# Layer-normed graph kernel of two layers: four small moves in the order of its first pairs and of its last one

## The chip, the cores and the metric

The kernel runs on one core of a Trainium2 chip. The metric is the device time of one execution in microseconds. Before the change it is 1700.62 us (median of three runs, 1700.39 to 1701.86).

## The reference, cut to what matters

There are 64 graphs of 256 nodes with 512 features, in fp32. Every graph uses the same adjacency matrix of zeros and ones, about 3% of them ones. Two layers follow each other; each normalises, clips at zero, mixes and adds to its input.

```python
# layer 0
h = maximum(layernorm(x), 0)
q, k, v = h @ Wq.T, h @ Wk.T, h @ Wv.T
rel = adj.T * (q @ k.T)                       # per graph, 256 x 256
rel = rel / norm(rel, axis=2, keepdims=True)
x = x + rel @ v
# layer 1
h = maximum(layernorm(x), 0)
x = x + (adj @ h) @ weight + bias
```

## The kernel before

**Tiling.** The graphs are worked in 32 pairs. A pair's x is one tile of 128 partitions by four chunks of 512 (two graphs, two halves of their nodes), 1 MB. Five such tiles form a ring (`x_ring`), so a pair's x is loaded several pairs ahead.

**Algebra.** Wq and Wk are folded into one matrix M once, in `before_pairs`, so that the scores are h M h transposed. Nearly all products are done by Strassen's scheme in Winograd's form: seven block products instead of eight, with sums of blocks formed ahead (`left_factors`, L176 to L179, and `right_operands`, L138 to L141) and added up afterwards. A product of blocks goes to one PSUM bank; its `take` copies it (ScalarE, first time) or adds it (VectorE) to the result. `bank_a` is used for several products one after the other; a product that starts `bank_a` afresh or goes on in it waits until the take before it has read the bank. `two_levels` goes one level deeper for some of the blocks (steps named a1, c5, a6, c, a7, a4 and g1 to g4).

**Before the pairs.** `before_pairs` loads adj, Wq and Wk, computes M from seven products and meanwhile prepares pair 0. With `early=True` the seven come in the order 1, 2, 5, 6, 3, 7, 4; they are called first to seventh product below, and the banks are a, b, c, a, c, a, a. The first and third, fourth and seventh are taken by ScalarE's copy, the second, fifth and sixth by VectorE's addition. The rest of the preparation is: the statistics of pair 0 (L333, L334), their root on ScalarE (L338), reciprocal and shift `nb` (L341, L342), four Relus into `blocks` (L345), and Wv turned by 16 transposes on TensorE into four banks (`transpose_wv`). After the branch on `low_any` (whether adj is exact in a shorter format, which it is here) pair 0's h is turned by 16 transposes (`transposes_by_matmul`), copied to `ht` by four copies of ScalarE (L434), and multiplied with M (`project_g`); the second product of that stage, in bank_c, needs L177, which needs all four copies.

**Order of the work.** TensorE, VectorE and ScalarE run in the order in which the program writes their instructions (`manual_schedule`). The order is laid out by hand: a dictionary `side` tells which small steps follow which product. `run_steps` runs product n and its take, then the steps listed under n. So an instruction on VectorE or ScalarE that must wait holds up all that is listed behind it. The order on GpSimd and SyncE (SP) is left to the scheduler; DMAs are issued from the queues of SP, ScalarE and GpSimd.

**Loads at the start.** SP issues Wq in four parts and then x of pair 0; ScalarE issues adj and then Wk in four parts. Wv is issued by ScalarE after the copy of the first product, x of pairs 1 and 2 later.

**Pairs 0 and 1.** `first_pairs` fills the pipeline. Its last stage runs `mix_and_v(0, ...)`: the product of pair 0's gathered h with the weight (steps of m, additions L786 and L537 to x) between products for pair 2. Meanwhile pair 1's scores, which sixteen small DMAs have placed by blocks of 32 (L592, `placed`), are turned by four transposes of VectorE (`turns`, L602), and L176 to L179 form sums of them for the attention of pair 1, which follows (`attend_and_v`, L675 and L682).

**The last pair.** `last_pairs` empties the pipeline. There the last pair's layer 1 is done while the pair before is mixed: Relus (L345), a split of h in two terms by ScalarE's cast (L720) and VectorE's subtraction (L724), the addition of the bias to x (`add_bias`, L736, four chunks on GpSimd), the gather with adj (`y_products`, L752, copied by L756) and the mixing with the weight. The bias may be added as soon as a chunk's Relu has read x, and must be there before the first L786 of that pair.

Of the kernel before, what the change touches and what calls it, by code (L numbers as in the profile page):

```python
# [19 lines left out]
def kernel(  # L20
# [38 lines left out]
    nc = tc.nc  # L59
    P = 128  # L60
    B, N, D = x.shape
# [38 lines left out]
    for e in range(DC):  # L100
        nc.sync.dma_start(out=wq_sb[:, e], in_=wq[e * P : (e + 1) * P, :])
        nc.scalar.dma_start(out=wk_sb[:, e], in_=wk[e * P : (e + 1) * P, :])
    load(0)
    ones = const.tile([P, 1], F32, name="ones")
# [625 lines left out]

    def add_bias(i):

        xt = flat(X[i])
        add = nc.gpsimd.tensor_tensor
        return [
            (lambda c=c: add(xt[:, c, :], xt[:, c, :], bias_bc, ALU.add)) for c in range(TC)  # L736
        ]
# [95 lines left out]
    def before_pairs():  # L833
# [36 lines left out]
        def transpose_wv():  # L870
            for d in range(DC):
                pt = ps_m.tile([P, 512], F32, tag="pm", name="ptw")
                for e in range(DC):
                    nc.tensor.transpose(pt[:, ts(e, P)], wv_sb[:, e, ts(d, P)], ident)
                if d < HC:
                    nc.scalar.copy(wvt_sb[:, d, :], pt[:, :D])
                else:
                    nc.vector.tensor_copy(wvt_sb[:, d, :], pt[:, :D])

        def take(t, k, bank, first):  # L880
# [11 lines left out]
            0: [load_wv, left_steps[2], right_steps[2]],  # L892
            1: [left_steps[3], left_steps[0]],
            2: [right_steps[0]] + stats[0:1] + [lambda: load(1, nc.scalar)],
            3: stats[1:4] + [root, lambda: load(2, nc.scalar)],
            4: [end] + relus + [right_steps[3]],
            5: m_steps[0:3] + [transpose_wv],
            6: m_steps[3:4],
# [48 lines left out]
    def first_pairs(exact):  # L947
# [50 lines left out]
        if exact:  # L998
# [14 lines left out]
            0: y_steps[2:4] + totals[0:2], 1: y_second[0:4] + totals[2:4],  # L1013
            2: y_second[4:8] + [mean] + row_squares[0:2], 3: v_steps[1:2] + row_squares[2:4],
            4: turns + rel_steps[0:2] + norm0[0:2], 5: rel_steps[2:4] + v_steps[2:3],
        })
# [51 lines left out]
    def last_pairs(exact, relu0, v_last, mixed, v):  # L1068
# [62 lines left out]
            0: [root], 1: y_second[0:4] + [end] + relus[0:2] + uppers[0:2], 2: y_second[4:8],  # L1131
            4: lowers[0:2] + relus[2:4], 5: uppers[2:4] + add_bias(c), 7: lowers[2:4],
        })
        y_products, y_steps = gather_steps(c, exact)
        run_steps(y_products, {0: [m["g4"]], 2: y_steps[0:1]})
        y_second = second_of_y(c, "hs2")
# [42 lines left out]
```

## Time and profile before

| | |
|---|---|
| median of three runs | 1700.62 us |
| the profiled execution's own time | 1700.89 us |
| its span, first to last instruction | 1699.1 us |
| TensorE, matmul busy | 1685.2 us (99%) |
| VectorE busy | 1474.9 us (87%) |
| ScalarE busy | 856.7 us (50%) |
| GpSimd busy | 227.1 us (13%) |
| TensorE busy, 0 to 30 us | 26.48 us |
| TensorE busy, 30 to 1610 us | 1578.31 us |
| TensorE busy, 1610 to 1699 us | 80.41 us |
| mean granted TensorE clock | 0.999 |

How to read it. The profile is of one execution, and durations and points in time are those of that execution; time counts from the start of its span. L12 is line 12 of the kernel before. Engines are PE (TensorE), PEld (its weight loads), DVE (VectorE), ACT (ScalarE), POOL (GpSimd) and SP; a q behind a name is that engine's queue, where it issues DMAs. A row of a timeline names the output and the input of an instruction. An fp32 matmul leaves two records, so a product of four matmuls is counted as x8. A wait is put down to what came last by semaphores. A busy TensorE is not one at its peak; the idle time between its instructions is what can be read for sure.

### The profile page before, as it was taken

To read this page: it belongs to the slowest core of one execution; us is meant where nothing else is said; L and a number is where in the kernel's file an instruction comes from. 1 tells how busy PE (TensorE), PEld (TensorE's weight loads), DVE (VectorE), ACT (ScalarE), POOL (GpSimd) and SP (SyncE) were. 2 spreads that over 40 slices of the span, in tenths; PEclk is the share of its full clock that TensorE was granted. 3 is DMA by queue.
4 is the path that set the end of the run, shared out by engine and by line. 5 is a ranking of instruction groups with operands and counts; after the bars stand their busy time and mean duration, and the time that the engine had idled before them with its cause. 6 is when DMAs were issued, how large, how long until landed. Compare 5 with 4: busy or idle time off the path is not lost.

```text
span 1699.1 us, 28457 instructions
## 1 busy us (share of the span) xinstructions
PE 1685.2 (99%) x10274; PEld 1530.6 (90%) x10274; DVE 1474.9 (87%) x3312; ACT 856.7 (50%) x1947; POOL 227.1 (13%) x191
## 2 busy tenths in 40 slices
PE   9999999999999999999999999999999999999998
PEld 7988999999999999999999999999999999999986
DVE  7788898888898888898888988888988889888777
ACT  4455445655545555446555456554465544564331
POOL 1211100111101111001111011110011110011111
PEclk9999999999999999999999999999999999999999
DMA  7413332233322233322333322333223333223101
GB/s 245 63 28 85 83 77 51 47 82 85 78 60 64 52 84 85 75 55 57 67 85 81 77 48 49 85 84 76 57 64 58 84 82 78 51 44 60 38 25 53
DMA packets 395270, 118.89 MB, mean 70 GB/s; under 512 B 367600, under 2 KB 368368, under 8 KB 395120
## 3 DMA queue, kind: packets, MB, share of 16 engines
q1 hardware_dynamic: 382528, 76.60, 24.1%
q0 software_dynamic: 8432, 32.51, 5.2%
q10 hardware_dynamic: 4160, 7.87, 1.3%
q8 instruction: 83, 1.36, 0.3%
q14 instruction: 67, 0.55, 0.1%
HBM read 38.27 MB, written 33.55 MB: 42 GB/s over the span
## 4 chain that ended last, share of the span: by engine, by line
PE 96%; DVE 3%; DMA 0%; issue 0%; ACT 0%; ACTq 0%; DVEq 0%
PE bank_a L302 25%; PE bank_a L290 13%; PE bank_a L314 7%; PE py L752 7%; PE bank_c L302 7%; PE bank_e L528 6%; PE bank_a L675 6%; PE bank_d L528 5%; PE bank_c L290 3%; PE bank_c L314 3%; PE bank_e L481 3%; PE bank_c L675 3%; PE bank_d L481 2%; PE bank_b L314 2%; PE bank_b L675 1%; PE pu L636 1%
## 5 line engine op out<-in xcount | busy, mean ns | idle before, releaser
L736 POOL TENSOR_TENSOR x_ring<-x_ring,bias_bc 128x512 f32<-128x512 f32 x128 | 187.6, 1486 | 667.6 <-DVE rel L563 436.3
L302 PE MATMUL bank_a<-wv_t,ht 128*128 128x256 f32 x768 | 181.7, 379 | 0.0
L290 PE MATMUL bank_a<-ht,m_t 128*128 128x256 f32 x768 | 181.4, 379 | 0.0
L290 PEld LDWEIGHTS bank_a<-ht,m_t 128*128 128x128 f32 x768 | 145.9, 190 | 19.8
L302 PEld LDWEIGHTS bank_a<-wv_t,ht 128*128 128x128 f32 x768 | 143.5, 190 | 18.3
L516 ACT COPY v<-bank_a 128x512 f32<-128x512 f32 x96 | 55.1, 574 | 206.5 <-PE bank_a L302 206.5
L724 DVE TENSOR_TENSOR h<-h2c,h 128x512 fp32r<-128x512 f32 x128 | 85.5, 691 | 80.1 <-ACT h L720 80.1
L367 ACT ACTIVATE blocks<-x_ring,sm 128x512 f32<-128x512 f32 x112 | 80.9, 722 | 119.4 <-DVE sm L364 117.6
L345 ACT ACTIVATE h2c<-x_ring,nb,rs 128x512 f32<-128x512 f32 x128 | 97.3, 808 | 59.7 <-DVE nb L342 50.0
L752 PE MATMUL py<-adjt_r,h 128*128 128x256 f32 x1024 | 126.0, 280 | 0.5 <-DVE h L724 0.4
L302 PE MATMUL bank_a<-w_t,ys 128*128 128x256 f32 x512 | 121.4, 380 | 0.4 <-DVE x_ring L786 0.3
L752 PEld LDWEIGHTS py<-adjt_r,h 128*128 128x128 f32 x1024 | 119.8, 188 | 1.0 <-DVE h L724 0.9
L807 POOL DMA_DIRECT2D out_dram<-x_ring x31 | 24.1, 776 | 720.5 <-issue 521.2
L380 ACT ACTIVATE h<-x_ring,nb,rs 128x512 f32<-128x512 f32 x112 | 82.0, 802 | 66.0 <-PE bank_e L528 66.0
L302 PEld LDWEIGHTS bank_a<-w_t,ys 128*128 128x128 f32 x512 | 96.8, 190 | 14.3 <-DVE x_ring L786 1.0
L786 DVE TENSOR_TENSOR x_ring<-bank_a,x_ring 128x512 f32<-128x512 f32 x128 | 88.0, 687 | 22.6 <-PE bank_a L302 22.5
L314 PE MATMUL bank_a<-ht,gt 128*128 128x128 f32 x744 | 101.2, 279 | 0.0
L561 ACT COPY rel<-bank_a 128x256 f32<-128x256 f32 x96 | 35.8, 373 | 129.7 <-PE bank_a L314 107.3
L333 DVE BATCH_NORM_STATS2 st<-x_ring 128x6 f32<-128x512 f32 x144 | 97.8, 679 | 0.4
L756 ACT COPY yt<-py 128x512 f32<-128x512 f32 x128 | 75.1, 588 | 45.4 <-PE py L752 44.5
L314 PEld LDWEIGHTS bank_a<-ht,gt 128*128 128x128 f32 x744 | 90.4, 192 | 3.0
L453 DVE STREAM_TRANSPOSE ht<-blocks 128x256 f32<-128x256 f32 x248 | 87.8, 409 | 0.8 <-DMA blocks<-h 0.8
(224 smaller groups left out, 4064.7 us busy)
## 6 DMA issues: line engine op xcount, KB each, us to landing
blocks<-h SPq DMA_DIRECT2D x496, 64.0 KB, 2.3
out_dram<-x_ring POOLq DMA_DIRECT2D x31, 1024.0 KB, 4.8
x_ring<-in_x_dram SPq DMA_DIRECT2D x28, 1024.0 KB, 5.7
placed<-rel SPq DMA_DIRECT2D x384, 32.0 KB, 2.0
x_ring<-in_x_dram ACTq DMA_DIRECT2D x4, 1024.0 KB, 5.4
wq_sb<-in_L_gnn_Wq_dram SPq DMA_DIRECT2D x4, 256.0 KB, 4.9
wk_sb<-in_L_gnn_Wk_dram ACTq DMA_DIRECT2D x4, 256.0 KB, 6.3
wv_sb<-in_L_gnn_Wv_dram ACTq DMA_DIRECT2D x1, 1024.0 KB, 5.8
```

The costliest lines, as they stand in the source:

```text
L290: nc.tensor.matmul(bank[:, e * HT_ : (e + 1) * HT_], right[n][:, d, ts(e, P)], left[n][:, d, :], start=(start and e == 0 and d == 0), stop ...
L302: nc.tensor.matmul(bank[:, b * HD : (b + 1) * HD], left[n][:, d, ts(b, P)], right[n][:, d, :], start=(start and b == 0 and d == 0), stop=( ...
L314: nc.tensor.matmul(bank[:, ts(b, P)], right[n][:, d, ts(b, P)], left[n][:, d, ts(b, P)], start=(start and b == 0 and d == 0), stop=(d == H ...
L333: nc.vector.bn_stats(st[:, c, :], src[:, c, :])
L345: nc.scalar.activation(dst, src[:, c, :], AF.Relu, bias=nb[:, c : c + 1], scale=rs[:, c : c + 1])
L453: nc.vector.transpose(ht[:, d, half].rearrange("p (b n) -> p b n", b=NB), by_half[:, :, half, d])
L528: nc.tensor.matmul(out, left[k][n], right[k][n], start=start, stop=True, skip_group_check=True)
L675: nc.tensor.matmul(bank[:, ts(b, HD)], left[n][:, b], right[n][:, b], start=(start and b == 0), stop=True, skip_group_check=True,)
L724: nc.vector.tensor_sub(dst[:, 1, c, :], whole_h[c], dst[:, 0, c, :].bitcast(F32))
L736: (lambda c=c: add(xt[:, c, :], xt[:, c, :], bias_bc, ALU.add)) for c in range(TC)
L752: nc.tensor.matmul(pm[:, d, :], left[:, b * NC + m, ts(d0 + d, P)], right, start=(n == 0), stop=(n == len(terms) - 1),)
L786: nc.vector.tensor_add(xt[block], bank.rearrange("p (b e) -> p b e", b=NB), xt[block])
```

## The change

Four things are moved, and no arithmetic changes.

- x of pair 0 is loaded from ScalarE's DMA queue, behind Wk, instead of from SP's, behind Wq.
- Wv's transposes and copies come after the fourth product of M instead of after the sixth, and all four copies are ScalarE's; two were VectorE's. The small steps around are listed anew: two chunks of statistics come earlier, `left_steps[0]` and `right_steps[0]` later, `right_steps[3]` ahead of `end` instead of behind the Relus.
- The turns of pair 1's scores stand in slot 3 of `mix_and_v(0, ...)`, ahead of the steps already there, instead of in slot 4.
- The last pair's bias is added by VectorE instead of GpSimd: two chunks after the first and two after the third step of the gather.

In the order of instructions, ScalarE has the load of x between Wk's last part and its table load. On VectorE the stream of `before_pairs` reads: second product's addition, L179, two chunks of statistics, L138, L176, two chunks, L337, fifth product's addition, L141, L341, L342, sixth product's addition, and then the sums of M. In pair 0 the four turns stand ahead of L135 and of the additions L786, L537, L490 and L518. For the last pair, two L736 stand between the last L537 of the pair before and L176, and two between L176 and L177.

```diff
@@ -100,7 +100,7 @@
     for e in range(DC):
         nc.sync.dma_start(out=wq_sb[:, e], in_=wq[e * P : (e + 1) * P, :])
         nc.scalar.dma_start(out=wk_sb[:, e], in_=wk[e * P : (e + 1) * P, :])
-    load(0)
+    load(0, nc.scalar)
     ones = const.tile([P, 1], F32, name="ones")
     nc.gpsimd.memset(ones, 1.0)
     warm = work.tile([P, P], F32, tag="turned", name="warm")
@@ -728,10 +728,10 @@
 
         return chunks, root, end, each(relu_of), each(upper), each(lower)
 
-    def add_bias(i):
+    def add_bias(i, engine=nc.gpsimd):
 
         xt = flat(X[i])
-        add = nc.gpsimd.tensor_tensor
+        add = engine.tensor_tensor
         return [
             (lambda c=c: add(xt[:, c, :], xt[:, c, :], bias_bc, ALU.add)) for c in range(TC)
         ]
@@ -872,10 +872,7 @@
                 pt = ps_m.tile([P, 512], F32, tag="pm", name="ptw")
                 for e in range(DC):
                     nc.tensor.transpose(pt[:, ts(e, P)], wv_sb[:, e, ts(d, P)], ident)
-                if d < HC:
-                    nc.scalar.copy(wvt_sb[:, d, :], pt[:, :D])
-                else:
-                    nc.vector.tensor_copy(wvt_sb[:, d, :], pt[:, :D])
+                nc.scalar.copy(wvt_sb[:, d, :], pt[:, :D])
 
         def take(t, k, bank, first):
             dst = m_sb[:, t * HC : (t + 1) * HC, k * HD : (k + 1) * HD]
@@ -890,11 +887,11 @@
         run([right_steps[1], left_steps[1]])
         winograd(product_weights_moving(m_left, m_factors), take, {
             0: [load_wv, left_steps[2], right_steps[2]],
-            1: [left_steps[3], left_steps[0]],
-            2: [right_steps[0]] + stats[0:1] + [lambda: load(1, nc.scalar)],
-            3: stats[1:4] + [root, lambda: load(2, nc.scalar)],
-            4: [end] + relus + [right_steps[3]],
-            5: m_steps[0:3] + [transpose_wv],
+            1: [left_steps[3]],
+            2: stats[0:2] + [right_steps[0], left_steps[0], lambda: load(1, nc.scalar)],
+            3: [transpose_wv] + stats[2:4] + [root, lambda: load(2, nc.scalar)],
+            4: [right_steps[3], end] + relus,
+            5: m_steps[0:3],
             6: m_steps[3:4],
         }, early=True)
 
@@ -1011,8 +1008,8 @@
         run(y_steps[1:2])
         mixed = mix_and_v(0, g, v, {
             0: y_steps[2:4] + totals[0:2], 1: y_second[0:4] + totals[2:4],
-            2: y_second[4:8] + [mean] + row_squares[0:2], 3: v_steps[1:2] + row_squares[2:4],
-            4: turns + rel_steps[0:2] + norm0[0:2], 5: rel_steps[2:4] + v_steps[2:3],
+            2: y_second[4:8] + [mean] + row_squares[0:2],
+            3: turns + v_steps[1:2] + row_squares[2:4], 4: rel_steps[0:2] + norm0[0:2], 5: rel_steps[2:4] + v_steps[2:3],
         })
         return norm0[2], v_steps[3:4], mixed, v
 
@@ -1129,10 +1126,11 @@
             m["g3"],
         ], {
             0: [root], 1: y_second[0:4] + [end] + relus[0:2] + uppers[0:2], 2: y_second[4:8],
-            4: lowers[0:2] + relus[2:4], 5: uppers[2:4] + add_bias(c), 7: lowers[2:4],
+            4: lowers[0:2] + relus[2:4], 5: uppers[2:4], 7: lowers[2:4],
         })
         y_products, y_steps = gather_steps(c, exact)
-        run_steps(y_products, {0: [m["g4"]], 2: y_steps[0:1]})
+        biases = add_bias(c, nc.vector)
+        run_steps(y_products, {0: [m["g4"]] + biases[0:2], 2: y_steps[0:1] + biases[2:4]})
         y_second = second_of_y(c, "hs2")
         run(y_steps[1:2])
         m = mix_by_two_levels(c)
```

## The prediction

> **What bounds the kernel now.** I read the chain of waits first. It gives TensorE 96% of the span, so a change counts only where it takes idle time out of TensorE or puts some in. The second view is what TensorE waited for:
>
> ```profile
> PE bank_e L528 <- DVE x_ring L537: 3.3, 3, 1.6
> PE bank_a L302 <- DMA wk_sb<-in_L_gnn_Wk_dram: 1.4, 1, 1.4
> ...
> PE bank_c L290 <- DVE ht L177: 0.4, 1, 0.4
> ```
>
> Between 30 and 1610 us it waited once (1.6 us, pair 0). The change therefore acts in three places only, and each is worked out from the timeline there. The start:
>
> ```profile
> 8.07 2.59 PE L302 MATMUL bank_a<-wk_sb,wq_sb 128*128 128x256 f32 x6 [1.36 <-DMA wk_sb<-in_L_gnn_Wk_dram]
> ...
> 10.70 0.39 ACTq L112 DMA_DIRECT2D wv_sb<-in_L_gnn_Wv_dram  x1
> ...
> 19.74 0.17 DVE L342 SCALAR_TENSOR_TENSOR nb<-mv,rs 128x4 f32<-128x4 f32 x1
> 19.76 1.91 PE L874 MATMUL ptw<-ident,wv_sb 128*128 128x128 f32 x16
> 19.82 0.68 DVE L135 TENSOR_TENSOR wk_t<-wk_sb,wk_t 128x512 f32<-128x512 f32 x1
> 19.94 2.93 ACT L345 ACTIVATE blocks<-x_ring,nb,rs 128x512 f32<-128x512 f32 x4 [0.68 <-DVE nb L342]
> ...
> 27.33 1.99 PE L290 MATMUL bank_c<-ht,m_sb 128*128 128x256 f32 x8 [0.44 <-DVE ht L177]
> ```
>
> A row is start, duration, engine, line, operation, output<-input, count, and idle time before it. From 8.07 to 26.7 TensorE has one piece of work behind the other (a four-matmul product, recorded as x8, takes 1.73 us). One wait at the front counts (the second quarter of Wk, landed 7.93) and one at the end (L177, 27.33). The chain tool names VectorE in between, but TensorE did not stand still there. The place in pair 0:
>
> ```profile
> 124.17 1.41 DVE L602 STREAM_TRANSPOSE turned<-placed 128x256 f32<-128x256 f32 x4
> ...
> 128.31 0.46 PE L528 MATMUL bank_e<-w_t,yt 128*128 128x128 f32 x2 [1.63 <-DVE x_ring L537]
> ...
> 130.81 1.13 PE L675 MATMUL bank_a<-placed,rel 128*128 128x256 f32 x4
> ```
>
> VectorE is behind by its four turns, and TensorE waits for the addition that frees bank_e. The end:
>
> ```profile
> 1668.11 2.68 POOL L736 TENSOR_TENSOR x_ring<-x_ring,bias_bc 128x512 f32<-128x512 f32 x2 [14.68 <-DVE ys L178]
> 1668.30 1.37 DVE L178 TENSOR_TENSOR ys<-ys 128x128 f32<-128x128 f32 x1
> ...
> 1669.71 1.24 DVE L179 TENSOR_TENSOR ys<-ys,ys 128x128 f32<-128x128 f32 x1
> ...
> 1676.20 1.81 DVE L724 TENSOR_TENSOR h<-h2c,h 128x512 fp32r<-128x512 f32 x2
> ```
>
> While GpSimd adds the bias, VectorE's operations of 0.28 us take 1.37 and 1.24, and the pair at 1676.20 takes 1.81 instead of 1.28. TensorE waits for what stands behind them: 1.42 us at 1671.33 (L537), and at 1677.46 and 1678.06 for the two L724. The last pair's first product with the weight starts at 1680.57.
>
> **What the Trainium skill says.** "SBUF — State Buffer", Who interferes with whom: a VectorE instruction with two inputs in SBUF contends with a GpSimd instruction that reads SBUF, and the loser blocks for the whole instruction. The trace agrees (1.37 against 0.28 us). "DMA: Bandwidth & Descriptors", Issuing engines are not separate DMA queues: loads of all issuing engines interleave on the same 16 DMA engines. The trace agrees: from 6 to 7 us the SP queue has 49.1% and the ACT queue 50.6%. "TensorE: Matmul & The Clock Gate", Part 1: the clock is halved after an idle window of about 3.4 us, and the window runs free of the kernel. The trace agrees: granted clock 0.50 from 9 to 11 us, each half matmul 0.43 instead of 0.22 us.
>
> **The change, part by part.**
>
> *Load of x0 on ScalarE's queue.* One issue of 0.39 us leaves SP at 3.63 (SP's next work is the branch at 24) and goes behind Wk's last issue on ScalarE, at about 4.65. Table load, root and adj copy move by 0.4 us; adj's first user is the mask at 57. Hidden. For Wk: the SP queue had sent Wq (1.05 MB) by about 7.8 us and up to 10 us some 0.5 MB of x0, so Wk's end should come 1.3 us sooner (0.5 MB at about 0.39 MB/us): landing 9.4, not 10.7. But TensorE's second product began at 10.46 because the first, at half clock, ended there; its third load was needed at 11.31. Only the second quarter (7.93) counts, and before 7.2 hardly any x0 moved. Value 0, bounds 0 and −1.3. x0 itself lands as before, near 12.3, since the sum of bytes is the same; its first use moves from 15.53 to 14.33. Hidden, with 2 us to spare.
>
> *Wv's 16 transposes ahead of the fifth product; order of steps.* TensorE's work is the same, its neighbours are not. In the new order VectorE's L342 (nb) stands behind the addition of the fifth product (bank_c), which now stands behind the transposes.
> - The fourth product ends at 16.30 as before. Wv's load is issued behind the first copy (10.70) and lands 5.8 later, at 16.5: wait 0.2. Transposes 16.55 to 18.28, fifth product to 20.01.
> - VectorE: addition from 20.26 (0.61 to the next), L141, now ahead of L341 (0.60), L341 and L342 (0.36): nb at 21.83, against 19.91. The four Relus, 2.93: ready at 24.8, against 22.87.
> - Sixth product 20.01 to 21.74. The seventh overwrites its bank: before, the transposes lay between and covered the addition (0.69); now TensorE waits for it, 21.95 to 22.64. Seventh product 22.68 to 24.41.
> - The first group of h's transposes needs the fourth Relu: done 24.9 instead of 23.66; all four 26.2. ScalarE copies m_sb at 24.7 (gone ahead: two wvt copies, which were in its way until 23.8) and ht from 25.2, 0.51 each, to 27.2; L177 from 27.25. It took 1.00 with GpSimd beside it, 0.69 without: bank_c of g starts at 27.98 to 28.3, against 27.33.
> - VectorE saves two copies (1.28), but they lay where it would have waited for ScalarE's m_sb (24.3 before, 25.3 after). Worth 0 here. left_steps[0] goes behind two stats and is needed at 20.0, done by 17.2: hidden. The load of x2 moves on ScalarE behind the copies, 19.06 to some 19.6; x2 is used at 40.85: hidden.
> Value +0.85 us. Bounds: +0.4 (no wait for Wv, short L177, two tenths at pt) and +1.2. TensorE runs without a gap from there to 126 us, so it stays.
>
> *Turns of pair 1 a slot sooner.* Four of 0.35 move ahead of L135, L786, L537, L490, L518 on VectorE, to 120.68. Their input: the last packets of placed moved before 119.0, so no wait. L786 of a7: 121.90 → 122.74, bank_a free at 123.42, product a4 123.03 → 123.46: a new wait of 0.43. Then L176 124.62 instead of 125.62; L372 to L377 include a wait for the root: 126.1; L786 126.14 instead of 127.15, L537 126.74 instead of 127.75. TensorE's 128.31 becomes 127.2 and its 130.81 becomes 129.8. Value −1.0; bounds −1.6 (the whole stall goes) and −0.5.
>
> *Last pair's bias by VectorE.* L178 and L179 take 0.28 each: L537 at 1668.82 instead of 1670.87, but the L786 behind waits for its product (1669.64 + 0.2): 1669.85 instead of 1671.53, −1.68. g2 no longer waits. Everything to 1675 shifts by that. Third and fourth L724: 1.28 instead of 1.81, so −2.2 at the end of the fourth. Added: four additions with two SBUF inputs, priced like L724 (0.69, 0.60 between starts): two at 1676.05 to 1677.25, when L176 would wait for ScalarE's copy until 1677.37; two at 1677.98 to 1679.18, when L177's copy arrives at 1679.18. Both pairs lie in waits (before: 1.22 and 1.12 us of idle), so they cost about 0; without that cover 2.4. GpSimd's store L807 of the pair before no longer stands behind L736; nobody waits for it. Value −2.2; bounds −2.5 and 0.
>
> *Sum.* +0.85 − 1.0 − 2.2 = −2.35. The profiled execution took 1700.89 (span 1699.1 and 1.8 around it), so 1698.54; the median is 0.27 lower: **1698.3 us**.
>
> **Rivals.**
> - *Wk frees the start.* If x0 did hold Wk's second quarter, the first product begins up to 1.3 us sooner and the idle window may not halve the clock. Wv's load then becomes the bound (issued about 1.3 sooner, behind x0), so I take −0.9 for the start instead of +0.85: −4.1, 1696.5. For it: TensorE's only DMA wait is there. Against it: the queue shares before 7.2 us.
> - *VectorE becomes the bound of the tail.* The four additions find no cover, +2.4 against −2.2: total about 0, 1700.5. For it: its idle there is exactly as long as they are. Against it: the copies it waits for come from TensorE and do not get sooner.
> - *Wv comes late (slower).* x0 is now ahead of it on ScalarE's ring. If Wv takes the place that x1 had (landing 14.79 + 5.4 = 20.2 instead of 16.5), fifth product, nb and Relus come 3.7 later: +1.35, 1702.0. It decides from a landing at about 18.9 on. Against it: in the trace x0's last packets go by 11.6, before Wv's first at about 11.9.
>
> **How the numbers follow.** Forecast 0.66 (own range 1697.2 to 1699.7), Wk 0.15, VectorE 0.12, Wv 0.07. The range 1696.4 to 1700.8 leaves out half of the first rival, the third and a little of the second. A measurement of this kernel tells 0.2% (3.4 us) from no change, which is below 1697.2 or above 1704.0: faster 0.20 (most of the first rival, the forecast's edge), slower 0.05, within 0.75.
>
> **What would show it.** Start: transposes of Wv at about 16.5, a wait of the seventh product on VectorE (0.9), nb near 21.8, bank_c of g near 28.2. Pair 0: the 1.63 gone to about 0.4 twice. Tail: L178 and L179 at 0.28, from there to the last instruction 2.2 us less than before. I am wrong if g's bank_c starts before 27.3 or after 29, or if L176 and L177 of the last pair wait behind L736.

## The result and the profile after

The changed kernel takes **1698.41 us** (median of 22 runs, 1697.05 to 1699.79). The kernel before, on the same chip, takes 1700.85 us (22 runs, 1700.39 to 1702.17). The ratio is 0.9985, with a 95% interval of 0.9978 to 0.9991: the change saves 2.4 us, which is less than the 0.2% (3.4 us) that the prediction called no change. The interval leaves out 1, so the saving is small but real.

| | before | after |
|---|---|---|
| the profiled execution's own time | 1700.89 us | 1699.60 us |
| its span | 1699.1 us | 1697.8 us |
| TensorE, matmul busy | 1685.2 us | 1687.27 us |
| VectorE busy | 1474.9 us | 1473.29 us |
| ScalarE busy | 856.7 us | 857.89 us |
| GpSimd busy | 227.1 us | 221.50 us |

The profiled execution of the changed kernel is 1.2 us above its median, and TensorE is busy for 2.1 us longer although it does the same work. Of these, 1.9 lie ahead of M's third product (11.71 us busy up to its start, 9.77 before), where matmuls ran at half rate for longer than before. That the 1.2 us have the same cause is likely and not shown. The half rate is taken up below.

What TensorE waited for in the changed kernel (total, times, longest, in us), the answer to the first view that the prediction shows:

```profile
PE bank_a L302 <- DVE m_sb L883: 0.8, 1, 0.8
PE bank_a L302 <- DMA wk_sb<-in_L_gnn_Wk_dram: 0.7, 1, 0.7
...
PE bank_e L528 <- DVE x_ring L537: 0.2, 1, 0.2
```

Of the three waits of bank_e, 3.3 us together, one of 0.2 is left. The waits of g's second product for L177 and of the gather for L724 (0.4 each) are gone from the list. A new one of 0.8 stands in it: M's seventh product waits for VectorE's addition of the sixth (L883 here, L886 before).

TensorE at the start, in the timeline of the changed kernel:

```profile
8.42 2.90 PE L302 MATMUL bank_a<-wk_sb,wq_sb 128*128 128x256 f32 x6 [0.68 <-DMA wk_sb<-in_L_gnn_Wk_dram]
11.11 3.31 PE L302 MATMUL bank_b<-wk_sb,wq_sb 128*128 128x256 f32 x8
14.26 1.89 PE L302 MATMUL bank_c<-wk_t,m_room 128*128 128x256 f32 x8
...
17.71 1.91 PE L874 MATMUL ptw<-ident,wv_sb 128*128 128x128 f32 x16
...
23.86 1.99 PE L302 MATMUL bank_a<-wk_t,wq_sb 128*128 128x256 f32 x8 [0.78 <-DVE m_sb L883]
25.69 2.00 PE L431 MATMUL pt<-ident,blocks 128*128 128x128 f32 x16
...
29.49 1.75 PE L290 MATMUL bank_c<-ht,m_sb 128*128 128x256 f32 x7
```

In the kernel before, M's second and third products stand at:

```profile
10.46 2.56 PE L302 MATMUL bank_b<-wk_sb,wq_sb 128*128 128x256 f32 x8
12.85 1.89 PE L302 MATMUL bank_c<-wk_t,m_room 128*128 128x256 f32 x8
```

Two things are to be seen. First, the product at 11.11 takes 3.15 us to the next, 2.39 before, where a full clock gives 1.73: matmuls run at half rate for longer than in the profile before, and M's third product starts at 14.26 instead of 12.85. Of these 1.41 us, 0.35 are a later second quarter of Wk (8.42 instead of 8.07), and 1.06 are slower matmuls in the first two products. Second, from that third product to g's second it is 15.23 us (14.26 to 29.49), against 14.48 before (12.85 to 27.33). Wv's transposes at 17.71 did not wait: Wv's load was issued at 11.36 and landed 5.1 us later.

VectorE in pair 0 and in the last pair, and then TensorE in pair 0, both from the timeline of the changed kernel:

```profile
122.79 1.41 DVE L602 STREAM_TRANSPOSE turned<-placed 128x256 f32<-128x256 f32 x4
...
1669.15 0.29 DVE L178 TENSOR_TENSOR ys<-ys 128x128 f32<-128x128 f32 x1
1669.47 0.29 DVE L179 TENSOR_TENSOR ys<-ys,ys 128x128 f32<-128x128 f32 x1
...
1675.48 1.28 DVE L724 TENSOR_TENSOR h<-h2c,h 128x512 fp32r<-128x512 f32 x2
...
1677.01 1.28 DVE L736 TENSOR_TENSOR x_ring<-x_ring,bias_bc 128x512 f32<-128x512 f32 x2
1678.32 0.69 DVE L176 TENSOR_TENSOR ys<-yt 128x512 f32<-128x512 f32 x1
1678.93 1.28 DVE L736 TENSOR_TENSOR x_ring<-x_ring,bias_bc 128x512 f32<-128x512 f32 x2
1680.14 0.69 DVE L177 TENSOR_TENSOR yt<-yt 128x512 f32<-128x512 f32 x1
```

```profile
122.09 1.89 PE L302 MATMUL bank_a<-w_t,ys 128*128 128x256 f32 x8
...
125.44 1.99 PE L302 MATMUL bank_a<-w_t,yt 128*128 128x256 f32 x8
...
129.24 0.46 PE L528 MATMUL bank_e<-w_t,yt 128*128 128x128 f32 x2
...
131.74 1.13 PE L675 MATMUL bank_a<-placed,rel 128*128 128x256 f32 x4
```

The first two of these products, in the kernel before:

```profile
119.97 1.89 PE L302 MATMUL bank_a<-w_t,ys 128*128 128x256 f32 x8
...
123.03 1.89 PE L302 MATMUL bank_a<-w_t,yt 128*128 128x256 f32 x8
```

The product at 129.24 has no wait in its row, where it had 1.63. Some 0.2 us of waiting are left all the same: it starts 1.08 us after the product ahead of it (L675 at 128.16), and the next product of that kind takes 0.87 to its follower (129.76 to 130.63). VectorE still sets the pace here. Its L537, which frees bank_e, begins 6.59 us after the product bank_a<-w_t,ys (at 128.68) instead of 7.78 (at 127.75), and this 1.19 us is all that TensorE gains in the stretch.

In the last pair, L178 and L179 take 0.29 instead of 1.37 and 1.24, the pair of L724 takes 1.28 instead of 1.81, and the two pairs of L736 fill VectorE's time without a row showing a wait. In the kernel before, VectorE stood idle there for ScalarE's copies:

```profile
1679.57 0.69 DVE L176 TENSOR_TENSOR ys<-yt 128x512 f32<-128x512 f32 x1 [1.22 <-ACT yt L756]
...
1681.38 0.69 DVE L177 TENSOR_TENSOR yt<-yt 128x512 f32<-128x512 f32 x1 [1.12 <-ACT yt L756]
```

**A ledger by stretches.** Points in time of single executions are shifted by whatever came earlier, so I cut each profiled execution at six instructions and compare the lengths between them. The cuts are the starts of M's third product (bank_c), of g's second product (bank_c), of the last product in pair 0 ahead of the place where the turns matter (bank_a<-w_t,ys, at 119.97 before), of the attention product bank_a<-placed,rel of pair 1, of the last mixing with the weight of the pair before the last (bank_a<-w_sb,yt), and of VectorE's last addition (L537). The stretch between the last two is called "end". All in us, one execution each.

| kernel | up to M's third | to g's second | to pair 0 | pair 0 | middle | end |
|---|---|---|---|---|---|---|
| before | 12.85 | 14.48 | 92.64 | 10.84 | 1530.39 | 32.33 |
| after | 14.26 | 15.23 | 92.60 | 9.65 | 1530.31 | 30.15 |
| difference | +1.41 | +0.75 | −0.04 | −1.19 | −0.08 | −2.18 |

The differences add up to −1.33, and the spans differ by 1.3. Without the first column they add up to −2.74, and the medians differ by 2.44.

### The profile page after: what moved, and what is told of

The parts are those of the page before. It is cut to its first block, busy times and chain, and to the rows that moved or that the text cites. A ratio compares the mean times of both kernels' runs of the same rounds, so it can differ in the third digit from the quotient of the medians.

```text
span 1697.8 us, 28452 instructions
## 1 busy us (share of the span) xinstructions
PE 1687.3 (99%) x10274; PEld 1531.7 (90%) x10274; DVE 1473.3 (87%) x3314; ACT 857.9 (51%) x1949; POOL 221.5 (13%) x187
## 3 DMA queue, kind: packets, MB, share of 16 engines
q8 instruction: 83, 1.36, 0.3%
## 4 chain that ended last, share of the span: by engine, by line
PE 96%; DVE 3%; DMA 0%; issue 0%; ACTq 0%; ACT 0%; DVEq 0%
PE bank_a L302 26%; PE bank_a L290 13%; PE bank_c L302 7%; PE bank_a L314 7%; PE py L752 7%; PE bank_e L528 6%; PE bank_a L675 6%; PE bank_d L528 5%; PE bank_c L290 3%; PE bank_c L314 3%; PE bank_e L481 3%; PE bank_c L675 3%; PE bank_d L481 2%; PE bank_b L314 2%; PE bank_b L675 1%; PE pu L636 1%
## 5 line engine op out<-in xcount | busy, mean ns | idle before, releaser
L736 POOL TENSOR_TENSOR x_ring<-x_ring,bias_bc 128x512 f32<-128x512 f32 x124 | 182.2, 1489 | 649.6 <-DVE rel L563 436.4
L724 DVE TENSOR_TENSOR h<-h2c,h 128x512 fp32r<-128x512 f32 x128 | 85.3, 689 | 80.1 <-ACT h L720 80.1
L786 DVE TENSOR_TENSOR x_ring<-bank_a,x_ring 128x512 f32<-128x512 f32 x128 | 88.0, 688 | 22.2 <-PE bank_a L302 22.1
```

The source lines that it names most:

```text
L724: nc.vector.tensor_sub(dst[:, 1, c, :], whole_h[c], dst[:, 0, c, :].bitcast(F32))
L786: nc.vector.tensor_add(xt[block], bank.rearrange("p (b e) -> p b e", b=NB), xt[block])
```

## The experiments

Every kernel was timed beside the kernel before. The medians of the kernel before in the four series of experiments were 1700.46, 1700.80, 1700.61 and 1700.46 us. The stretches of each experiment's profiled execution:

| kernel | up to M's third | to g's second | to pair 0 | pair 0 | middle | end |
|---|---|---|---|---|---|---|
| e1_tail | 14.29 | 14.47 | 92.63 | 10.84 | 1530.15 | 30.16 |
| e2_turns | 12.15 | 14.48 | 92.80 | 9.65 | 1530.28 | 32.38 |
| e3_x0 | 10.92 | 14.47 | 92.69 | 10.84 | 1530.45 | 32.31 |
| e4_wv | 14.61 | 15.24 | 92.67 | 10.84 | 1530.21 | 32.31 |
| f0_fill | 11.63 | 14.48 | 93.08 | 10.84 | 1530.20 | 32.32 |
| f1_fill_after | 11.49 | 16.22 | 92.61 | 9.64 | 1530.01 | 30.16 |
| f2_fill_old_start | 12.60 | 14.48 | 92.63 | 9.64 | 1530.12 | 30.16 |
| f3_fill_old_x0 | 11.01 | 14.47 | 92.98 | 9.65 | 1530.33 | 30.17 |
| g1_no_bias | 11.12 | 14.49 | 92.67 | 9.64 | 1530.12 | 30.15 |
| g2_split_fill | 11.76 | 15.14 | 92.75 | 9.64 | 1530.33 | 30.16 |
| g3_old_start | 11.93 | 14.47 | 92.84 | 9.64 | 1530.15 | 30.15 |
| h1_fill_wv | 11.75 | 15.23 | 93.06 | 10.84 | 1530.09 | 32.33 |

### One part alone: e1 to e4

Each is the kernel before with one of the four parts of the change.

**e1_tail**, the last pair's bias by VectorE:

```diff
...
-            4: lowers[0:2] + relus[2:4], 5: uppers[2:4] + add_bias(c), 7: lowers[2:4],
+            4: lowers[0:2] + relus[2:4], 5: uppers[2:4], 7: lowers[2:4],
...
-        run_steps(y_products, {0: [m["g4"]], 2: y_steps[0:1]})
+        biases = add_bias(c, nc.vector)
+        run_steps(y_products, {0: [m["g4"]] + biases[0:2], 2: y_steps[0:1] + biases[2:4]})
```

> Only the last pair's bias is moved to VectorE. Ledger theory (each part is worth what its own stretch of the trace shows): 2.2 us less than the kernel before, L178 and L179 at 0.28 us instead of 1.37 and 1.24, and the four L736 inside VectorE's waits for ScalarE's copies. Rival (VectorE becomes the bound of the tail): the four additions cost their 2.4 us, so no change within 0.5 us.

Measured: 1698.54 us (21 runs, 1697.60 to 1699.99), ratio 0.999 [0.9983, 0.9996], that is 1.9 us less. The end takes 30.16 us instead of 32.33, as in the whole change.

**e2_turns**, the turns of pair 1's scores a slot sooner:

```diff
-            2: y_second[4:8] + [mean] + row_squares[0:2], 3: v_steps[1:2] + row_squares[2:4],
-            4: turns + rel_steps[0:2] + norm0[0:2], 5: rel_steps[2:4] + v_steps[2:3],
+            2: y_second[4:8] + [mean] + row_squares[0:2],
+            3: turns + v_steps[1:2] + row_squares[2:4], 4: rel_steps[0:2] + norm0[0:2], 5: rel_steps[2:4] + v_steps[2:3],
```

> Only the four turns of pair 1 stand a slot sooner. Ledger theory: 1.2 us less than the kernel before; TensorE's wait of 1.63 us for L537 goes, about 0.3 us come back where the product a4 waits for the addition of a7. Rival (the wait is only moved to the next bank): within 0.4 us of the kernel before.

Measured: 1699.11 us (13 runs, 1698.95 to 1700.93), ratio 0.9994 [0.9985, 1.0002], 1.35 us less. By the median alone this would not be settled. The stretch "pair 0" settles it: 9.65 instead of 10.84, and it is 9.64 or 9.65 in the changed kernel and the seven experiments with this part, and 10.84 in the kernel before and the five experiments without it.

**e3_x0**, x of pair 0 on ScalarE's queue:

```diff
-    load(0)
+    load(0, nc.scalar)
```

> Only x of pair 0 goes to ScalarE's queue, behind Wk. Ledger theory: no change within 0.5 us, since TensorE waits for the second quarter of Wk alone, which is sent before x0's bytes move; Wk's last quarter lands about 1 us sooner and nobody waits for it. First rival (Wk frees the start): 1 us less or more than that, with the first product of M beginning before 7.5 us. Second rival (the longer stretch at half clock in the changed kernel's profile comes from this move): about 1.4 us more than the kernel before, in every execution.

Measured: 1700.05 us (13 runs, 1698.63 to 1702.65), ratio 0.9999 [0.999, 1.0007]: no difference that these runs can show, with a spread of 4 us. The profiled execution happened to run at full clock from the start, and M's third product started at 10.92. So this run alone cannot tell a gain by the load from a lucky clock.

**e4_wv**, Wv's transposes behind the fourth product, with all four copies on ScalarE (as in the change, left out here) and the new list of steps:

```diff
...
-            1: [left_steps[3], left_steps[0]],
-            2: [right_steps[0]] + stats[0:1] + [lambda: load(1, nc.scalar)],
-            3: stats[1:4] + [root, lambda: load(2, nc.scalar)],
-            4: [end] + relus + [right_steps[3]],
-            5: m_steps[0:3] + [transpose_wv],
+            1: [left_steps[3]],
+            2: stats[0:2] + [right_steps[0], left_steps[0], lambda: load(1, nc.scalar)],
+            3: [transpose_wv] + stats[2:4] + [root, lambda: load(2, nc.scalar)],
+            4: [right_steps[3], end] + relus,
+            5: m_steps[0:3],
...
```

> Only Wv's transposes, their copies and the order of the steps around M are changed; x of pair 0 stays on SP's queue. Ledger theory: 0.65 us more than the kernel before; from the start of M's third product to the start of the second product of g 15.1 us instead of 14.5, with TensorE waiting 0.8 to 0.9 us ahead of M's last product. Rival (the longer stretch at half clock comes from this order): about 2 us more. Second rival (the two copies taken from VectorE pay for the order): no more than the kernel before.

Measured: 1702.04 us (13 runs, 1700.95 to 1703.22), ratio 1.0008 [1.0, 1.0017], 1.6 us more. The profiled execution is the slowest of the 13 (1703.22). Its trace shows half of the 1.6 in the place that the part touches (15.24 instead of 14.48, +0.76). The rest of the difference in span lies ahead of M's third product, which starts at 14.61:

```profile
11.22 3.55 PE L302 MATMUL bank_b<-wk_sb,wq_sb 128*128 128x256 f32 x8
14.61 1.89 PE L302 MATMUL bank_c<-wk_t,m_room 128*128 128x256 f32 x8
...
24.21 1.99 PE L302 MATMUL bank_a<-wk_t,wq_sb 128*128 128x256 f32 x8 [0.78 <-DVE m_sb L883]
```

Up to there its instructions on TensorE are those of the kernel before. What differs is the rate: the second product takes 3.39 us to the next (11.22 to 14.61) instead of 1.73. So the first four runs left two questions: is the start's first column chance, and what does each part of the start do when the clock is full?

### The clock taken out: f0 to f3

These four kernels give TensorE more to do ahead of M's first product: one more warming matmul at the beginning and four between adj's transposes and M. What they compute is not used.

```diff
-        for _ in range(8):
+        for _ in range(9):
...
         transpose_adj()
+        for _ in range(4):
+            nc.tensor.matmul(pz[:, :P], warm, warm, start=True, stop=True)
```

f0_fill is the kernel before with them, f1_fill_after the changed kernel with them. f2_fill_old_start has them, the turns and the tail, and the start otherwise as before. f3_fill_old_x0 is f2 with x of pair 0 on ScalarE's queue.

> The kernel before with nine instead of eight warming matmuls and four more of them between adj's transposes and M's first product, where TensorE waits for Wk; their result is not used. Ledger theory: nothing else changes, TensorE stays at full clock from then on, M's third product starts at about 12.0 us (Wk's last quarter is then the bound), and the executions lie within about 1 us of one another; 0.5 us less than the kernel before. Rival (the half clock at the start has nothing to do with TensorE's idle time): the same spread and the same median as the kernel before, or up to 1 us more for the added matmuls.

> The changed kernel with the same thirteen warming matmuls. Ledger theory: M's third product at about 11 us, since Wk's last quarter now lands sooner; Wv lands at about 14.8 us, 0.4 us after M's fourth product has ended, so its transposes wait for that; from M's third product to g's second 15.1 us and this wait. Together 3.5 to 4 us less than the kernel before. Rival (the clock is not held): as the changed kernel, 2.4 us less.

> The warming matmuls, the turns and the bias as in the changed kernel; the start as before (x of pair 0 on SP's queue, Wv's transposes behind M's sixth product). Ledger theory: M's third product at about 12.0 us, from there to g's second 14.5 us; 3.4 us less than the kernel before with the warming matmuls alone. Rival (the new order of the start is worth its while at full clock): at least 0.5 us slower than the changed kernel with the warming matmuls.

> As the run before it, and x of pair 0 on ScalarE's queue behind Wk: all of the changed kernel but the new place and copies of Wv's transposes, with the warming matmuls. Ledger theory: M's third product at about 10.9 us, so that moving x of pair 0 is worth 1 us once TensorE is at full clock; from there to g's second product 14.5 us; about 4.5 us less than the kernel before and 0.7 to 1.1 us less than the changed kernel with the warming matmuls. Rival (x of pair 0 is worth nothing at any clock): as the run before it, within 0.3 us.

Measured:

| kernel | median us (runs) | lowest to highest | ratio to before |
|---|---|---|---|
| f0_fill | 1700.29 (13) | 1699.87 to 1701.07 | 0.9996 [0.9988, 1.0004] |
| f1_fill_after | 1697.31 (12) | 1696.57 to 1698.20 | 0.9978 [0.9970, 0.9987] |
| f2_fill_old_start | 1696.79 (9) | 1696.28 to 1697.34 | 0.9976 [0.9966, 0.9986] |
| f3_fill_old_x0 | 1696.25 (7) | 1695.41 to 1696.39 | 0.9971 [0.9959, 0.9982] |

In all four the third product starts between 11.01 and 12.60. M's products run at full clock or nearly so (1.73 to 2.00 us where none waits for Wk). In f0, f1 and f2 adj's transposes ahead of them still run at half rate (404 to 421 ns each, 273 in f3), so there the clock comes up only after them. The medians of the kernel before and f0 can't be told apart.

What the load of x0 does at full clock is seen between f2 and f3. First f2, then f3, both TensorE:

```profile
11.20 1.56 PE L302 MATMUL bank_b<-wk_sb,wq_sb 128*128 128x256 f32 x6 [0.83 <-DMA wk_sb<-in_L_gnn_Wk_dram]
12.60 1.89 PE L302 MATMUL bank_c<-wk_t,m_room 128*128 128x256 f32 x8
```

```profile
9.28 1.89 PE L302 MATMUL bank_b<-wk_sb,wq_sb 128*128 128x256 f32 x8
11.01 1.89 PE L302 MATMUL bank_c<-wk_t,m_room 128*128 128x256 f32 x8
```

With x0 on SP's queue the second product waits 0.83 in its middle for Wk; with x0 behind Wk it doesn't wait. The third product starts 1.59 sooner. Of that, 1.13 lies in the second product (9.74 to 12.60 against 9.28 to 11.01: the wait and getting under way again), and 0.46 ahead of it, of which the load explains at most 0.11 (a wait of the first product for Wk of 0.28 against 0.17). The medians differ by 0.54, less than their intervals.

The wait for Wk's last quarter goes with the queue. It stands in all three traces with the extra matmuls and x0 on SP's queue (0.59 in f0, 0.83 in f2, 0.45 in h1 below) and in none of the four with x0 behind Wk (f1, f3, g1, g2). The 1.59, though, is the difference of the two that lie furthest apart. With x0 on SP's queue the third product starts at 11.63, 12.60 and 11.75, with x0 behind Wk at 11.49, 11.01, 11.12 and 11.76, which is 0.65 sooner on average. The latest of the four, g2, waited 1.02 for Wk's second quarter.

In f1, the changed kernel at full clock, some of it is given back. TensorE is now early enough to wait for Wv:

```profile
15.88 1.97 PE L874 MATMUL ptw<-ident,wv_sb 128*128 128x128 f32 x16 [0.77 <-DMA wv_sb<-in_L_gnn_Wv_dram]
...
22.08 1.99 PE L302 MATMUL bank_a<-wk_t,wq_sb 128*128 128x256 f32 x8 [0.78 <-DVE m_sb L883]
```

Wv was issued at 9.84, behind the first product's copy, and landed 6.0 us later. So 16.22 in the second stretch is 14.48, plus the 0.75 of the new order, plus about 1.0 of waiting for Wv. f2 and f3, which leave Wv's transposes in the old place, don't have either.

### What the start's cost consists of, and the cover of the bias: g1 to g3

**g1_no_bias** is f3 without the four additions of the last pair's bias.

```diff
-        biases = add_bias(c, nc.vector)
-        run_steps(y_products, {0: [m["g4"]] + biases[0:2], 2: y_steps[0:1] + biases[2:4]})
+        run_steps(y_products, {0: [m["g4"]], 2: y_steps[0:1]})
```

> The kernel of f3_fill_old_x0 (M's products as before, x of pair 0 on ScalarE's queue, turns a slot sooner, thirteen warming matmuls), and the bias of the last pair left out altogether, so nobody adds it. My theory: VectorE's four additions lie in waits for ScalarE's copies and cost nothing, so this kernel needs as long as f3_fill_old_x0 within 0.4 us, about 4.5 us less than the kernel before; ScalarE's last copies, L176, L177 and the product behind them come at the same distance from the end of the stage before, and VectorE shows idle time of about 1.2 us ahead of L176 and 1.1 ahead of L177 in the place of the additions. Rival (VectorE is the bound of the tail): they cost up to 2.4 us there, and this kernel is 1 to 2.4 us shorter than f3_fill_old_x0.

Measured: 1696.12 us (8 runs, 1695.59 to 1696.51), ratio 0.9975 [0.9964, 0.9985]; f3 has 1696.25. The end takes 30.15 us, with the additions 30.17. VectorE in g1, in the place of the additions:

```profile
1674.32 0.69 DVE L176 TENSOR_TENSOR ys<-yt 128x512 f32<-128x512 f32 x1 [1.23 <-ACT yt L756]
1676.13 0.69 DVE L177 TENSOR_TENSOR yt<-yt 128x512 f32<-128x512 f32 x1 [1.12 <-ACT yt L756]
```

Where the additions are left out, VectorE stands still for 1.23 and 1.12 us, waiting for ScalarE's copies. The four additions lie in that time and cost nothing.

**g2_split_fill** is f1 with two things mended in the start: nb ahead of the fifth product's addition, and half of Wv's transposes back between the sixth and the seventh product.

```diff
-        def transpose_wv():
-            for d in range(DC):
+        def transpose_wv(part):
+            for d in part:
...
-            3: [transpose_wv] + stats[2:4] + [root, lambda: load(2, nc.scalar)],
-            4: [right_steps[3], end] + relus,
-            5: m_steps[0:3],
+            3: [lambda: transpose_wv(range(0, HC))] + stats[2:4] + [root, end, lambda: load(2, nc.scalar)],
+            4: [right_steps[3]] + relus,
+            5: m_steps[0:3] + [lambda: transpose_wv(range(HC, DC))],
```

> The changed kernel with thirteen warming matmuls (as f1_fill_after), and two things in M's products put differently: the shift of pair 0's statistics (L341, L342) ahead of the fifth product's addition, and half of Wv's transposes between the sixth and the seventh product. My theory of the start's cost (0.65 to 0.75 us): it comes from the seventh product, which waits 0.78 for VectorE's addition that the transposes used to cover, and from the Relus behind a late nb. Then the wait of 0.78 is gone or under 0.1, nb comes 2 us sooner, and from M's third product to g's second it takes 14.5 plus the wait for Wv (0.8 to 1.0), that is 15.3 to 15.5 instead of 16.2; the time is 0.7 us less than that of f1_fill_after. Rival (only Wv's landing costs, the rest is the copies of four transposes on ScalarE): the sum stays near 16.2, because the copies of the second half hold up m_sb or ht, and the time stays.

Measured: 1696.83 us (13 runs, 1695.88 to 1698.24), ratio 0.9976 [0.9967, 0.9984]; f1 has 1697.31. The trace shows it more clearly than the medians. TensorE in g2:

```profile
15.94 1.09 PE L874 MATMUL ptw<-ident,wv_sb 128*128 128x128 f32 x8 [0.56 <-DMA wv_sb<-in_L_gnn_Wv_dram]
...
21.27 1.99 PE L302 MATMUL bank_a<-wk_t,wq_sb 128*128 128x256 f32 x8
```

The seventh product waits no longer. From the third product to g's second it takes 15.14, in which the wait for Wv is still contained. Counted by lengths, as in f1, that wait is 0.78: 0.72 from the end of the fourth product (15.22) to the first transpose, and 0.06 in getting under way. Without it 14.36 are left, no more than the old order's 14.48. So the cost of the new order is the lost cover and the late nb together. They were mended at once, and this run doesn't divide the cost between them. Wv's landing is a cost of its own, which g2 keeps.

**g3_old_start** is the change without its two parts at the start (turns and tail alone, no warming matmuls added).

> The change without its two parts at the start: x of pair 0 on SP's queue and Wv's transposes where they were; turns a slot sooner and the last pair's bias by VectorE stay; no warming matmuls. My theory: turns 1.2 and tail 2.2 add up, 3.4 us less than the kernel before, less than what the changed kernel gains (2.4); from M's third product to g's second 14.48, and the half-clock stretch ahead of it as chance has it. Rival (the parts at the start bring time at half clock): no more than 2.4 us less than before.

Measured: 1697.26 us (12 runs, 1696.54 to 1698.01), ratio 0.998 [0.9971, 0.9988], 3.35 us less than before. This is the sum that turns and tail should give (1.19 + 2.18). It is 0.9 us more than the whole change saves, though the intervals of the two ratios overlap.

### The excess of e4: h1

**h1_fill_wv** is e4 with the warming matmuls, to see whether the excess of 0.8 us ahead of the third product goes with the clock.

> The kernel before with thirteen warming matmuls and, of the change, only the new place of Wv's transposes and copies (as e4_wv, which took 1.6 us more than before where the trace of the start gives 0.65 to 0.75). My theory: what e4_wv took beyond that is the half-clock stretch ahead of M's third product, so with the warming matmuls the new order costs 0.65 to 0.75 from M's third product to g's second, and beside it a wait for Wv of 0 to 0.8 us (its load is issued behind the first product at about 9 and lands some 5.9 later, the transposes are due at about 15.1). Sum: 0.65 to 1.5 us over f0_fill's 1700.3, so 1700.9 to 1701.8, M's third product at 11.5 to 12.0. Rival: the new order itself costs 1.6 or more, ahead of the third product too; then that product starts later than 12.3 although the clock is full, or the distance from it to g's second is above 16.1.

Measured: 1700.90 us (13 runs, 1700.51 to 1701.15), ratio 1.0 [0.9992, 1.0009]. The third product starts at 11.75 and g's second 15.23 later:

```profile
15.20 1.91 PE L874 MATMUL ptw<-ident,wv_sb 128*128 128x128 f32 x16
...
21.35 1.99 PE L302 MATMUL bank_a<-wk_t,wq_sb 128*128 128x256 f32 x8 [0.78 <-DVE m_sb L883]
```

The new order costs 0.75 here as in the changed kernel, without a wait for Wv, and the excess ahead of it is gone with the half clock. M's second product waits 0.45 for Wk here, as it does in f0 and f2. h1 lies 0.6 us above f0, or 0.95 when each is set against the kernel before of its own series. This fits e4's 1.6 us being about half the new order and half a longer half-clock stretch. Only one execution of e4 was traced, though, and why its 13 runs should on average have met a longer stretch than those of the kernel before is not shown.

## Why the prediction held, and where its terms were off

The prediction said 1698.3 us and 1698.41 were measured. Its sum of three terms was −2.35, and the three measure −2.62.

**Start, +0.85 forecast, +0.75 measured.** The mechanism was as described: the seventh product waits for VectorE (0.9 forecast, 0.94 between the end of the sixth and its start), nb comes late, and L177's wait shrinks. The terms are to be read in the timelines: 0.94 for the seventh product, 0.1 each ahead of h's transposes and of g's first product (1.83 and 1.84 from the product before instead of 1.73 and 1.75), less 0.39 because g's second product now follows 1.96 behind the first instead of 2.35. That makes 0.74, and the stretch has 0.75. What failed is the 0.2 for Wv. In the profiled execution Wv landed at 16.46 and was needed at 17.71, because the slower start had moved TensorE by 1.41 and Wv's issue by 0.66 only (10.70 to 11.36). At full clock the wait exists and is larger than forecast: 0.77 in f1. One of the signs of being wrong that the prediction named did come up: g's bank_c starts at 29.49, after its 29. This is the later third product again. Without those 1.41 us it is 28.08 (forecast 28.2), and nb is ready at 21.62 (forecast 21.83).

**Pair 0, −1.0 forecast, −1.19 measured.** The mechanism was right, and its size was a little off. The turns now lie where VectorE had waited for TensorE, 0.54 at L786 (121.90) and 0.31 at L490 (123.23), so all that follows on VectorE comes sooner. What was mis-sized is by how much: on the time scale of the kernel before, the L537 that frees bank_e was put at 126.74 and began at 126.56. TensorE waits for VectorE twice, as forecast. The new wait ahead of the product bank_a<-w_t,yt was put at 0.43; it is 0.29 (from the product bank_a<-w_t,ys to it 3.35 us, 3.06 before), and 0.1 is lost in getting under way. At bank_e some 0.2 are left of the 1.63, where 0.4 were forecast.

**The last pair, −2.2 forecast, −2.18 measured.** L178, L179 and the L724 take what they take without GpSimd beside them. This is the contention that the Trainium skill describes in "SBUF — State Buffer", Who interferes with whom, and the trace agrees from the other side: with GpSimd's L736 out of the stretch, 0.29 in place of 1.37 and 1.24. How long the two were held up can be read in the kernel before: GpSimd's first addition ends at 1669.52 and L178 at 1669.67, GpSimd's second at 1670.79 and L179 at 1670.95. Each of VectorE's two ends 0.15 or 0.16 us after one of GpSimd's, so each sat out a whole addition. That the four additions cost nothing was the step with the largest bound (2.4 us), and g1 shows it.

**Load of x0, 0 forecast.** Right for executions in which M's first product runs at half clock (in none of the six traces of that kind does the second product wait for Wk), wrong for the others. The step that failed is the one that the second product "began at 10.46 because the first, at half clock, ended there": it took the clock of one execution for the kernel's. At full clock Wk is what the second product waits for, 0.83 in f2, 0.59 in f0 and 0.45 in h1, and not in f3.

**The conversion to the median.** The prediction set the profiled execution 0.27 above the median and moved it as a whole. The start of an execution differs by more than that from one to the next. In the seven profiled executions without extra matmuls (before, after, e1 to e4 and g3), M's third product starts between 10.92 and 14.61, though TensorE's instructions up to there are the same. The range had no term for this. That the forecast came within 0.1 us is partly luck. Its terms together saved 0.27 too little; the start and pair 0 were off in the same direction. Against that, the median that it started from was 0.23 too low (1700.62 of three runs, 1700.85 of 22), and 0.18 of what the stretches save is not in the medians (2.62 and 2.44). These nearly cancel.

**The rivals.**
- *Wk frees the start* was right that x0 can hold Wk up, and wrong about where. It expected the second quarter to come sooner and with it the first product. What x0 delays is the last quarter, which the second product waits for, and only at full clock. The wait for the second quarter shows no such gain: with the extra matmuls it is at most 0.29 with x0 on SP's queue and up to 1.02 (g2) behind Wk. Its value, −0.9 for the start instead of +0.85, is in no run: f1 has the sooner third product (11.49) and then loses 1.7 us to the new order and to Wv, as the rival itself feared.
- *VectorE becomes the bound of the tail* falls with g1.
- *Wv comes late* did not come true: Wv landed 5.1 us after its issue in the changed kernel and 6.0 in f1, against 5.8 before. Its price of 3.7 us for nb is in no run. What is left of it is the wait of 0.77.

For the parts of the start taken together the forecast of +0.85 holds in medians too: without the extra matmuls they cost about 1 us (1697.26 without these parts, 1698.41 with them, in separate series). So the change is probably better without them, though the intervals of the two ratios overlap. The version that keeps the load and drops the new order of Wv's transposes, f3, is the fastest of the kernels that do the whole work: 1696.25 us, ratio 0.9971 [0.9959, 0.9982], 4.55 us below the kernel before and 1.06 below f1. Its interval overlaps with those of f1 and f2, so that it beats the kernel before is shown, and that it beats f2 is only in the trace. The load of x0 behind Wk with the old order and without the extra matmuls was not run.

## What to carry to other kernels

When TensorE is busy for 99% of the span, cut two profiles at the same instructions and compare the lengths of the stretches: 0.75, 1.19 and 2.18 us come out the same to some hundredths in every trace that has the part in question and no wait for Wv, in kernels whose medians differ by as much as their noise. Before moving work away from between two dependent instructions, ask what it was covering; sixteen transposes hid VectorE's addition of 0.69, and moving them turned it into a wait. Work may be given at no cost to an engine that waits for something else, if the wait is in the profile and what it waits for does not depend on that work.

## What was unexpected of the hardware

The stretch at half clock at the start differs from one execution to the next. The second product of M, 1.73 us at full clock, took 2.39 in the profiled execution before, 3.15 in the one after, 3.39 in e4 and 1.73 in e3. The Trainium skill says in "TensorE: Matmul & The Clock Gate", Part 1, that the activity window runs free of the kernel, and so that the number of slow matmuls changes from run to run. The traces agree that it changes: e3 and e4 reach M's third product 3.7 us apart, of which 0.7 is a later Wk and 3.0 are slower matmuls. That is more than the change under study is worth.

The durations show more than a fall of the clock. The warming matmuls take 421 ns in all fourteen traces (the median of each), and the same matmul takes 275 ns when it is repeated just ahead of M in f0. So every execution begins at half rate. In the changed kernel and in e1 no matmul runs at full rate until the end of M's second product: as far as the durations tell, the clock had not come up yet. In the kernel before and in e4 adj's transposes already run at full rate (273 ns, 421 in the changed kernel), and M's first product is back at half rate after pauses of TensorE of at most 1.36 and 1.75 us. The prediction names an idle window of about 3.4 us as what halves the clock, and the profile before in agreement; the halving is there, but no pause of that length stands between the first matmuls in any of these traces, so what sets the moment stays open.

With five extra matmuls of one tile each, M's products ran at full clock or nearly so in all seven traces, and without them in one of seven (e3). Whether the extra matmuls bring the clock up sooner or keep it up is not separated. The runs of six of these kernels lie within 0.6 to 1.6 us of each other, and those of g2 within 2.4; without them it is 1.5 us in g3, 2.0 to 4.0 in e1 to e4, and 2.7 in the changed kernel. So a narrower spread is likely, and not shown.

The column of the granted clock is not enough to see this. It shows 0.50 from 9 to 11 us in the kernel before and 1.00 there in the changed kernel, while both ran their matmuls at half rate. The first row is from the kernel before, the second from the changed one:

```profile
9.00:11.00 2.00, 2.00 (x6) 1.53 (x6) 1.62 (x3) 0.30 (x1) 0.00 (x0) 0.50 1.05 406
9.00:11.00 2.00, 2.00 (x6) 1.62 (x5) 1.49 (x4) 0.00 (x0) 0.00 (x0) 1.00 1.01 383
```

A row has the stretch, its length, busy time and count of TensorE, its weight loads, VectorE, ScalarE and GpSimd, granted clock, DMA share and GB/s. Both have six records of half matmuls in 2 us, with TensorE busy all the time; in e3, at full clock, the same stretch has eleven. In both kernels the slow matmuls of M take 631 ns and their weight loads some 333, where they take 379 and 190 at full rate. That the clock is the cause in the changed kernel too is inferred from this likeness. The starts of the matmuls tell the rate, and here the column did not.
